# An RWKV time-mix stage in a whole-network kernel: one batch's recurrence levels issued between the last rounds of the stage before, the other's between outputs

## The chip, the cores and the metric

The kernel runs on one core of one Trainium2 chip. It computes a whole small network in one launch. The metric is the device time of that launch in microseconds (us), as the median of several runs. The core has TensorE (PE in the profile; PEld is its weight load), VectorE (DVE), ScalarE (ACT), GpSimd (POOL) and SyncE (SP, which here only issues DMAs). Each engine takes its own instructions strictly in the order in which they were built; engines wait for one another by semaphores.

## The reference, cut to what matters

The network is four residual blocks. The change lies in the first: an adapter with layer norm, then the RWKV time mix for 2 batches of 1024 tokens, 256 channels, 4 heads of 64. Everything is float32.

```
xx = shift(x) - x
m  = tanh((x + xx*maa_x) @ w1)                     # 4 x 32 wide
xw, xk, xv, xr = x + xx*(maa_f + m[f] @ w2[f])     # f in w, k, v, r
r, k, v = xr @ W_r, xk @ W_k, xv @ W_v
w = exp(-exp(decay + tanh(xw @ dw1) @ dw2))
# per head, over the tokens:
y_t = r_t @ (S + u * k_t v_t^T)
S   = diag(w_t) S + k_t v_t^T
out = groupnorm(y) @ W_o
x   = x + out
```

After it come a conditioned feed-forward layer ("cond2"), a mixture of experts, and two further blocks; they are not touched.

## The kernel before

**The front** is `tmix_in` (L261 to L375). The 2048 tokens are four chunks of 512 (`NCK` = 4, `CK` = 512); chunks 0 and 1 are batch 0, chunks 2 and 3 batch 1. Three generators work on a chunk: `adapt` (adapter and layer norm), `mix` (the four mixed inputs) and `project` (r, k, v and the decay w). Round i runs `adapt` on chunk i, `mix` on chunk i-1 and `project` on chunk i-2, and `together` (L253) takes their steps in the order of a string written out by hand:

```
together("apmpapmppaamppp", **steps)
```

So round 4 has only the mix of chunk 3 and the projection of chunk 2, and round 5 only the projection of chunk 3. r, k and v of batch 0 are complete after round 3. In `mix`, DVE multiplies each mixed input (L310) and POOL adds to it (L311), 4 of each for either half of the channels. In `project` the matmuls stand at L320 (decay), L328 (k and r), L336 (decay, second) and L346 (v); the front's PSUM is the pool "adp" (two banks "ad", one "nv", one "pa") and "mxp" (four banks f0 to f3).

**The recurrence** is `wkv` (L378 to L586). Each batch is cut into 8 pieces of 128 tokens. Within a piece the decayed products of r and k are built as a tree: a diagonal (L406; matmuls L414, times a mask by DVE at L422; its r is scaled by u on ACT at L560), then six levels with blocks of 1 to 32 tokens (L424). A level is 64 matmul instructions on 64x64 quarters of the array with 32 columns (L434, two records each in the profile). Its result is copied into A by DVE with a mask for levels 0 to 3 (L447, two copies of 512 columns per level), by ACT for levels 4 and 5 (L454). After each level comes a decay step (L456): POOL multiplies half of k (L462), DVE multiplies half of r (L463) and the running products `tot` (L465). The next level of the same batch needs the multiplied k and r. After the six levels `last` (L468) does the step between the two halves of a piece (matmuls L474, copies L482), with a decay as well. The two batches take turns at every level:

```
for l in range(6):
    for b in range(B):
        level(pp, b, l)
        decay(sp, b, l)
```

The levels use four PSUM banks named "sc".

**States and outputs.** `states` transposes k (L492, copied by ACT at L495), makes the state products (L509, copied at L516), and scans over the 8 pieces on DVE (L519). `output` (L522) makes y for two pieces at a time from A and v (L531) and from r and the states (L542); ACT copies one half out (L553), DVE adds the other (L554). `tmix_out` (L589) works on a chunk: square (L597), its sums (L602), the inverse root spread out (L607, L613), the normalized tile yn (L620, L621), and the output projection W_o (L626) added to x (L627). Its steps are taken in turn with the outputs, two steps after each. States of both batches come first, then the outputs of batch 0, then those of batch 1.

**After it** comes `cond2_0` (L635); its first matmul is at L654. Its weights, and those of the experts and their biases (L932), are loaded by DMAs that SP issues in the order of the program, each as soon as the memory that it writes is free.

Of the kernel before, what the change touches and what calls it, by code (L numbers as in the profile page):

```python
# [9 lines left out]
F32 = mybir.dt.float32  # L10
# [79 lines left out]
def setup(k, ctx):  # L90
    nc, tc, ins = k.nc, k.tc, k.ins
    cp = ctx.enter_context(tiles(tc, name="const", bufs=1))
    k.vecs = cp.tile([P, NVEC], F32, name="vecs")
    nc.sync.dma_start(out=k.vecs, in_=ins["vecs"])
    k.ident = cp.tile([P, P], F32, name="ident")
    make_identity(nc, k.ident)
    k.avg = cp.tile([P, P], F32, name="avg")
    nc.vector.memset(k.avg, 1.0 / C)

    k.sel64 = cp.tile([P, 2], F32, name="sel64")  # L100
    nc.vector.memset(k.sel64, 0.0)
    for h in range(2):
        nc.vector.memset(k.sel64[64 * h : 64 * h + 64, h : h + 1], 1.0 / 64)
    k.ones = cp.tile([P, P], F32, name="ones")
    nc.vector.memset(k.ones, 1.0)
    k.eps = {}
    for n, e in (("ln", 1e-5), ("gn", 0.00064)):
        k.eps[n] = cp.tile([P, 1], F32, name=f"eps_{n}")
        nc.vector.memset(k.eps[n], e)
# [134 lines left out]
def adapted(k, sp, pp, x, it, tables, names, hid):  # L244

    q = it["q"] = sp.tile([P, 2, CK + 1], F32, name="q", bufs=2)
    if it["ch"] % 2:
        k.nc.vector.tensor_copy(q[:, :, 0:1], it["prev"]["q"][:, :, CK : CK + 1])
    else:
        k.nc.vector.memset(q[:, :, 0:1], 0.0)  # L250
    yield from adapter_steps(k, sp, pp, x, it["ch"], q[:, :, 1:], tables, names, hid)
# [9 lines left out]
def tmix_in(k, x, r, kk, w, v):  # L261
# [10 lines left out]
    with (  # L272
# [4 lines left out]

        centre_weights(k, sp, ap, k.d0, D0, "wu", "bu")
# [4 lines left out]
        def adapt(it):  # L283
            return adapted(k, sp, ap, x, it, (k.d0, D0), ("wd", "wu", "bd", "bu"), P)
# [82 lines left out]
        for i in range(NCK + 2):  # L367
# [7 lines left out]
            together("apmpapmppaamppp", **steps)  # L375


def wkv(k, r, kk, w, v, y, x):  # L378
# [7 lines left out]
    NC = S // P  # L386
    M = NC - 1
    H = P // 2
    halves = [slice(i * H, i * H + H) for i in range(2)]
    with (  # L390
        tiles(tc, name="wka", bufs=1) as ap,
        tiles(tc, name="wkq", bufs=1, space=PSUM) as qp,
    ):
        eye = ap.tile([P, H], F32, name="eye")
        nc.vector.tensor_add(eye, k.ident[:, 0:H], k.ident[:, H:P])


        A = [ap.tile([P, 2, 2, NC, P], F32, name=f"A{b}") for b in range(B)]
        tot = [w[b].rearrange("p c t -> p (c t)") for b in range(B)]
        for b in range(B):  # L400
            nc.gpsimd.memset(A[b][halves[1], :, :, :, H:P].rearrange("p a c n t -> p (a c n) t"), 0.0)

        def bank(pp, shape):
            return pp.tile(shape, F32, name="sc", bufs=4)

        def diagonal(pp, b, ru):  # L406

            for c in range(2):
                ps = [bank(pp, [P, NC, H]) for par in range(2)]
                for ck in range(NC):  # L410
                    for half in range(2):
                        ts = slice(ck * P + half * H, ck * P + (half + 1) * H)
                        for par in range(2):
                            nc.tensor.matmul(  # L414
                                ps[par][halves[half], ck, :],
                                lhsT=kk[b][halves[par], c, ts],
                                rhs=ru[halves[par], c, ts],
                                start=True,
                                stop=True,
                            )  # L420
                for par in range(2):
                    nc.vector.tensor_mul(A[b][:, par, c, :, 0:H], ps[par], eye.unsqueeze(1).to_broadcast([P, NC, H]))  # L422

        def level(pp, b, l):  # L424

            h = 1 << l
            ps = [bank(pp, [P, 2, NC, H // 2]) for par in range(2)]
            for c in range(2):
                for ck in range(NC):
                    for half in range(2):  # L430
                        ts = slice(ck * P + half * H, ck * P + (half + 1) * H)
                        for par in range(2):
                            rv = r[b][halves[par], c, ts].rearrange("p (n two h) -> p n two h", two=2, h=h)
                            nc.tensor.matmul(  # L434
                                ps[par][halves[half], c, ck, :],
                                lhsT=kk[b][halves[par], c, ts],
                                rhs=rv[:, :, 1, :],
                                start=True,
                                stop=True,
                            )  # L440
            for par in range(2):
                dv = A[b][:, par, :, :, 0:H].rearrange("p c n t -> p (c n) t")
                dv = dv.rearrange("p g (n two h) -> p g n two h", two=2, h=h)[:, :, :, 1, :]
                pv = ps[par].rearrange("p c n t -> p (c n) t").rearrange("p g (n h) -> p g n h", h=h)
                if h < 16:
                    m = k.lvl[:, l].rearrange("p g (n h) -> p g n h", h=h)
                    nc.vector.copy_predicated(dv, m, pv)  # L447
                    continue

                for s0 in range(0, P, 32):  # L450
                    n = (s0 % H) // (2 * h)
                    if s0 % (2 * h) < h:
                        ss = slice(s0, s0 + min(h, 32))
                        nc.scalar.copy(dv[ss, :, n, :], pv[ss, :, n, :])  # L454

        def decay(sp, b, l):  # L456
            h = 1 << l
            n = 2 * S // (2 * h)
            t2 = tot[b].rearrange("p (n two) -> p n two", two=2)
            kv = kk[b].rearrange("p c (n two h) -> p (c n) two h", two=2, h=h)  # L460
            rv = r[b].rearrange("p c (n two h) -> p (c n) two h", two=2, h=h)
            nc.gpsimd.tensor_mul(kv[:, :, 0, :], kv[:, :, 0, :], t2[:, :, 1].unsqueeze(2).to_broadcast([P, n, h]))  # L462
            nc.vector.tensor_mul(rv[:, :, 1, :], rv[:, :, 1, :], t2[:, :, 0].unsqueeze(2).to_broadcast([P, n, h]))  # L463
            nt = sp.tile([P, n], F32, name=f"tot{l}", bufs=2)
            nc.vector.tensor_mul(nt, t2[:, :, 0], t2[:, :, 1])  # L465
            tot[b] = nt

        def last(pp, b):  # L468

            for c in range(2):  # L470
                ps = [bank(pp, [P, NC, H]) for par in range(2)]
# [11 lines left out]
            decay(ap, b, 6)  # L483

        def states(sp, b):
            kt = sp.tile([P, NC, C], F32, name="kt", bufs=1)
# [16 lines left out]
            pd = sp.tile([P, 2, H, M], F32, name="pd", bufs=1)  # L503
            for c in range(2):
                pu = qp.tile([P, NC, H], F32, name="pu")
# [16 lines left out]
        def output(sp, b, st, n):  # L522
# [28 lines left out]
            for a in range(2):  # L551
                t = sp.tile([P, 2, 2, H], F32, name="half")
# [3 lines left out]
        with tiles(tc, name="wks", bufs=2) as sp, tiles(tc, name="wkp", bufs=1, space=PSUM) as pp:  # L556
            for b in range(B):
                ru = sp.tile([P, 2, S], F32, name="ru")
                for c in range(2):
                    nc.scalar.activation(ru[:, c, :], r[b][:, c, :], AF.Copy, scale=k.vec("u", c))  # L560
                diagonal(pp, b, ru)
            for l in range(6):
                for b in range(B):
                    level(pp, b, l)
                    decay(sp, b, l)
            for b in range(B):
                last(pp, b)
        with (
            tiles(tc, name="wkt", bufs=2) as sp,
# [4 lines left out]
            before = [states(sp, b) for b in range(B)]  # L574
            left = []
            for b in range(B):
                for n in range(0, NC, 2):
                    output(sp, b, before[b], n)
                    for _ in range(2):
                        if left and next(left[0], 1):  # L580
                            left.pop(0)
                    if n % 4 == 2:
                        left.append(outs[(b * S + n * P) // CK])
            for steps in left:
                for _ in steps:
                    pass  # L586


def tmix_out(k, sp, pp, y, x, ch):  # L589
# [33 lines left out]
    for c in range(2):  # L623
        po = pp.tile([P, CK], F32, name="pw", bufs=2)
# [1164 lines left out]
def program(ctx: ExitStack, tc: tile.TileContext, ins, out):  # L1789
# [16 lines left out]
    with tiles(tc, name="w0", bufs=1) as wp:  # L1806
        load_adapter0(k, wp)
        with tiles(tc, name="rkwv", bufs=1) as ap:
            r, kk, w = ([ap.tile([P, 2, S], F32, name=f"{n}{b}") for b in range(B)] for n in "rkw")
            v = ap.tile([P, NBLK, C], F32, name="v")  # L1810
            with tiles(tc, name="zero", bufs=1) as zp:
# [11 lines left out]
                tmix_in(k, x, r, kk, w, v)  # L1823
            with tiles(tc, name="y0", bufs=1) as yp:
                y = yp.tile([P, 2, T], F32, name="y")
                wkv(k, r, kk, w, v, y, x)
# [138 lines left out]
```

## Time and profile before

| | |
|---|---|
| median of 3 runs | 1532.18 us (1529.52 to 1533.71) |
| the profiled execution | 1528.16 us |
| its span, first instruction to last | 1526.4 us |
| mean granted clock of PE | 0.959 |
| PE busy | 1426.0 us (93%) |
| DVE busy | 873.0 us (57%) |
| ACT busy | 680.4 us (45%) |
| POOL busy | 180.0 us (12%) |

A row of the profile's table of groups gives line, engine, operation, output and inputs by name, shape and count; then busy time and mean ns of one; then the idle time of the engine ahead of the group and what ended most of it. A line of the timeline gives start, duration, and the same; in brackets the idle time just before. "issue" is time for which no wait is seen. The granted clock is the share of full speed that PE was allowed. PE was at 1.00 from 50.7 us to 149.69, at 0.50 to 197.48, and at 1.00 to 224.79.

### The profile page before, as it was taken

Reading aid. Unit: us, or ns where it says so; the run is one execution under the profiler, and the core shown is the slowest. Engines: PE = TensorE matmul, PEld = TensorE weight load, DVE = VectorE, ACT = ScalarE, POOL = GpSimd, SP = SyncE. Lnnn points to the kernel's source line nnn. Section 1 sums busy time; section 2 is a strip of 40 time slices with the busy share of each in tenths; the row PEclk is TensorE's granted clock in tenths of the full one; section 3 lists DMA queues with packets and bytes.
Section 4 is the critical chain, followed back from the end, with each engine's and each line's share of the span. In section 5 each row is a group of like instructions: output and inputs, shape, how many; then the busy total and the mean of one; then the engine's idle time right before and its main releaser. Section 6 shows DMA issues by size and latency. Waiting matters only on the chain. (4 is left out here: it accounts for less than half of the span.)

```text
span 1526.4 us, 27470 instructions
## 1 busy us (share of the span) xinstructions
PE 1426.0 (93%) x10842; PEld 977.2 (64%) x10842; DVE 873.0 (57%) x2774; ACT 680.4 (45%) x1681; POOL 180.0 (12%) x167
## 2 busy tenths in 40 slices
PE   5998989999699999959999989999999999999998
PEld 2445977445456766736666545788887557878866
DVE  3545743121489921167888612788784237878764
ACT  2433242222122122127888621666574337656733
POOL 1533620022311111100000010000000000000011
PEclk9999589999799999979999999999999999999999
DMA  9500005200343342030000020000000000000001
GB/s 300 191 1 2 5 2 166 111 29 30 102 161 119 121 139 69 21 117 1 2 2 2 2 84 0 1 2 2 2 2 1 0 1 2 2 2 2 2 15 42
DMA packets 42759, 70.79 MB, mean 46 GB/s; under 512 B 7168, under 2 KB 35840, under 8 KB 39552
## 3 DMA queue, kind: packets, MB, share of 16 engines
q1 hardware_dynamic: 35776, 55.55, 10.9%
q0 software_dynamic: 3072, 8.65, 1.6%
q10 hardware_dynamic: 3776, 4.75, 1.0%
q8 instruction: 88, 1.44, 0.4%
q14 instruction: 47, 0.39, 0.1%
HBM read 45.09 MB, written 23.86 MB: 45 GB/s over the span
## 5 line engine op out<-in xcount | busy, mean ns | idle before, releaser
L1624 ACT ACTIVATE pe<-pe,nm 128x320 f32<-128x320 f32 x256 | 141.8, 555 | 131.2 <-DVE nm L1614 131.0
L1614 DVE CUSTOM_DVE_ANT_0 pe<-ps,wbs 128x320 f32<-128x320 f32 x256 | 118.6, 487 | 6.1 <-PE ps L1608 1.8
L1236 ACT ACTIVATE pe<-pe,nm 128x256 f32<-128x256 f32 x256 | 110.4, 498 | 20.4 <-DVE nm L1226 20.4
L971 PE MATMUL ph<-xt,w 128*128 128x512 f32 x256 | 113.8, 602 | 2.7 <-ACT xt L966 2.7
L1604 PE MATMUL ps<-kT,qT 64*128 64x384 f32 (+1 forms) x512 | 110.2, 498 | 3.4 <-DVE qT L1578 2.9
L979 PE MATMUL po<-w,h 128*128 128x256 f32 x512 | 111.8, 379 | 0.0
L979 PEld LDWEIGHTS po<-w,h 128*128 128x128 f32 x512 | 97.3, 190 | 16.6 <-issue 3.1
L1226 DVE CUSTOM_DVE_ANT_0 pe<-ps,lc 128x256 f32<-128x256 f32 x256 | 94.2, 417 | 20.9 <-PE ps L1210 19.3
L1673 PE MATMUL py<-ptt,v 128*64 128x128 f32 x1408 | 103.6, 277 | 0.1
L901 DVE SCALAR_TENSOR_TENSOR lc<-iok,idx,lc 128x256 f32<-128x256 f32 x248 | 102.3, 478 | 0.3
L971 PEld LDWEIGHTS ph<-xt,w 128*128 128x128 f32 x256 | 48.5, 193 | 62.7 <-issue 55.8
L1673 PEld LDWEIGHTS py<-ptt,v 128*64 128x64 f32 x1408 | 78.7, 137 | 11.1 <-issue 8.3
L1646 PE MATMUL pt<-ident,pe 128*128 128x128 f32 x512 | 79.8, 281 | 1.9 <-DVE pe L1632 0.9
L1245 PE MATMUL ptp<-ident,pe 128*128 128x128 f32 x512 | 73.7, 283 | 5.7 <-ACT pe L1236 3.1
L1245 PEld LDWEIGHTS ptp<-ident,pe 128*128 128x128 f32 x512 | 55.8, 142 | 33.1 <-ACT pe L1236 16.8
L974 ACT ACTIVATE h<-ph,vecs 128x512 f32<-128x512 f32 x64 | 44.0, 687 | 72.0 <-PE ph L971 71.0
L1633 ACT ACTIVATE pe<-pe,rd 128x320 f32<-128x320 f32 x128 | 70.7, 558 | 9.0 <-DVE rd L1631 8.9
L1608 PEld LDWEIGHTS ps<-sk,qT 64*128 64x128 f32 x512 | 50.9, 187 | 26.1 <-issue 0.3
L1505 PE MATMUL pq<-c,w1ak 128*128 128x512 f32 x128 | 61.7, 625 | 5.3 <-ACTq L1850 5.3
L1653 DVE TENSOR_TENSOR ptt<-pt,tri 128x512 f32<-128x512 f32 x96 | 64.9, 676 | 0.0
L1646 PEld LDWEIGHTS pt<-ident,pe 128*128 128x128 f32 x512 | 56.2, 141 | 10.9 <-issue 2.0
L982 DVE TENSOR_TENSOR ye<-po,b 128x256 f32<-128x256 f32 x32 | 13.4, 420 | 81.7 <-PE po L979 81.7
(355 smaller groups left out, 2764.7 us busy)
## 6 DMA issues: line engine op xcount, KB each, us to landing
w<-in_mw SPq DMA_DIRECT2D x16, 1024.0 KB, 5.1
xs<-z SPq DMA_DIRECT2D x8, 1088.0 KB, 11.8
ys<-z SPq DMA_DIRECT2D x4, 1024.0 KB, 11.6
xe<-xs SPq DMA_DIRECT2D x7, 544.0 KB, 6.2
more<-xs SPq DMA_DIRECT2D x7, 544.0 KB, 5.5
x<-in_xT ACTq DMA_DIRECT2D x4, 512.0 KB, 6.3
g<-ys ACTq DMA_DIRECT2D x4, 512.0 KB, 6.3
out_x<-o SPq DMA_DIRECT2D x8, 256.0 KB, 2.1
```

Of the source, the lines that this page charges most:

```text
L901: nc.vector.scalar_tensor_tensor(n, key, k.idx[:, qb, j : j + 1], n, ALU.is_equal, ALU.add)
L971: nc.tensor.matmul(ph, lhsT=w1[:, c, m * P : (m + 1) * P], rhs=xt[:, c, :], start=c == 0, stop=c == 1)
L979: nc.tensor.matmul(po, lhsT=h[:, m, j * P : (j + 1) * P], rhs=w2[:, m, :], start=m == 0, stop=m == 7)
L1226: nc.vector.tensor_tensor_reduce(out=pe[:, j, :], in0=it["ps"][i][:, j, :], in1=k.lc[:, q0 + j, :], scale=-1.0, scalar=3.0e38, op0=ALU.add ...
L1236: nc.scalar.activation(pe[:, j, :], pe[:, j, :], AF.Exp, bias=nm, scale=-1.0)
L1245: nc.tensor.transpose(ptp[:, kb, j, :], it["pe"][i][:, j, kb * P : (kb + 1) * P], k.ident)
L1604: nc.tensor.matmul(ps[:, i, keys[i]], lhsT=qs[i], rhs=kT[hp, m + pair, k0 : k0 + nk], start=True, stop=True)
L1614: nc.vector.tensor_tensor_reduce(out=pe[:, i], in0=ps[:, i, used[i]], in1=wbs[:, 0 if n == 0 else 3 if n == NB - 1 else 1 + i, (1 - i) * G ...
L1624: nc.scalar.activation(pe[:, i], pe[:, i], AF.Exp, bias=nm[:, i : i + 1], scale=-1.0, accum_out=den[:, i : i + 1])
L1633: nc.scalar.activation(pe[:, 1], pe[:, 1], AF.Copy, scale=rd[:, 1:2])
L1646: nc.tensor.transpose(pt[1 - j if i and inner(n) else j][:, 2 * pair + i, :], pe[:, at : at + P], k.ident)
L1673: nc.tensor.matmul(py[64 * i : 64 * i + 64, (m + pair) % 4, :], lhsT=keys[:, hs], rhs=it["pts"][:, pair, :] if j == 3 else it["pt"][:, j, ...
```

## The change

- The front takes steps of batch 0's recurrence as a fourth generator, `w`, in rounds 4 and 5, with an order of its own for each. Eight steps in all: two halves of the diagonal, six levels. They use the adapter's two "ad" banks, and the adapter's scratch memory is given up for the generator's `ru` and `tot` at round 4.
- In `wkv` only batch 1's levels are left. The first three steps (diagonal, diagonal, level 0) come first, then `last` of batch 0, level 1, `states` of batch 0, and then levels 2 to 5, each followed by one output of batch 0. Then come `last`, `states` and the outputs of batch 1.
- "sc" has two banks where it had four; the state products share the bank "pk" with the transposes; the output projection's "pw" has one bank where it had two. The scratch of states has one buffer where it had two, and batch 1's `ru` lies in the second half of y.
- The products `tot` alternate between w's memory and one more buffer, and stand right behind each level's decay.
- The small matrix `eye` is made at the start; A of batch 0 is allocated and cleared ahead of the front.

```diff
-def tmix_in(k, x, r, kk, w, v):
+def tmix_in(k, x, r, kk, w, v, A):
...
-        centre_weights(k, sp, ap, k.d0, D0, "wu", "bu")
+        beside = ExitStack()
+        dp = beside.enter_context(tiles(tc, name="ads", bufs=1))
+        centre_weights(k, dp, ap, k.d0, D0, "wu", "bu")
...
-            together("apmpapmppaamppp", **steps)
+            if i < NCK:
+                together("apmpapmppaamppp", **steps)
+                continue
+            if i == NCK:
+                beside.close()
+                dp = beside.enter_context(tiles(tc, name="wk0", bufs=1))
+                ru, tot = dp.tile([P, 2, S], F32, name="ru"), dp.tile([P, S], F32, name="tot")
+                levels = wkv_levels(k, r[0], kk[0], w[0], A, ru, tot, lambda shape: ap.tile(shape, F32, name="ad", bufs=2))
+            together("pwmpwmpwmpwppwpp" if i == NCK else "pwpwpwppppp", w=levels, **steps)
+        beside.close()
+def wkv_decay(k, r, kk, bufs, l):
+    nc = k.nc
+    h = 1 << l
+    n = 2 * S // (2 * h)
+    t2 = bufs[l % 2][:, 0 : 2 * n].rearrange("p (n two) -> p n two", two=2)
...
+    nc.gpsimd.tensor_mul(kv[:, :, 0, :], kv[:, :, 0, :], t2[:, :, 1].unsqueeze(2).to_broadcast([P, n, h]))
+    nc.vector.tensor_mul(rv[:, :, 1, :], rv[:, :, 1, :], t2[:, :, 0].unsqueeze(2).to_broadcast([P, n, h]))
+    nc.vector.tensor_mul(bufs[(l + 1) % 2][:, 0:n], t2[:, :, 0], t2[:, :, 1])
+def wkv_levels(k, r, kk, w, A, ru, tot, bank):
...
+    for c in range(2):
+        nc.scalar.activation(ru[:, c, :], r[:, c, :], AF.Copy, scale=k.vec("u", c))
+    for c in range(2):
...
+        yield
+    for l in range(6):
...
+        wkv_decay(k, r, kk, (w.rearrange("p c t -> p (c t)"), tot), l)
+        yield
...
+        def bank(shape):
+            return lp.tile(shape, F32, name="sc")
...
-                pu = qp.tile([P, NC, H], F32, name="pu")
+                pu = qp.tile([P, NC, H], F32, name="pk")
...
-        with tiles(tc, name="wks", bufs=2) as sp, tiles(tc, name="wkp", bufs=1, space=PSUM) as pp:
-            for b in range(B):
-                ru = sp.tile([P, 2, S], F32, name="ru")
-                for c in range(2):
-                    nc.scalar.activation(ru[:, c, :], r[b][:, c, :], AF.Copy, scale=k.vec("u", c))
-                diagonal(pp, b, ru)
-            for l in range(6):
-                for b in range(B):
-                    level(pp, b, l)
-                    decay(sp, b, l)
-            for b in range(B):
-                last(pp, b)
...
-            before = [states(sp, b) for b in range(B)]
...
+            ru = y[:, :, S : 2 * S]
+            levels = wkv_levels(k, r[1], kk[1], w[1], A[1], ru, ap.tile([P, S], F32, name="tot"), bank)
             for b in range(B):
+                for _ in range(3):
+                    next(levels, 1)
+                last(b)
+                next(levels, 1)
+                st = states(sp, b)
                 for n in range(0, NC, 2):
-                    output(sp, b, before[b], n)
-                    for _ in range(2):
-                        if left and next(left[0], 1):
-                            left.pop(0)
+                    next(levels, 1)
+                    output(sp, b, st, n)
+                    rest(2)
                     if n % 4 == 2:
                         left.append(outs[(b * S + n * P) // CK])
...
-        po = pp.tile([P, CK], F32, name="pw", bufs=2)
+        po = pp.tile([P, CK], F32, name="pw")
```

The bodies of the diagonal and of a level in `wkv_levels` are those of `diagonal` and `level` before.

## The prediction
> **What bounds the kernel now.** I read the page first, for where TensorE (PE) is not busy or not at full clock. The rows are tenths in 40 slices of 38.2 us:
>
> ```profile
> PE   5998989999699999959999989999999999999998
> PEclk9999589999799999979999999999999999999999
> ```
>
> PE is the bound nearly everywhere. The lowest clock of the whole span is in the fifth slice (152.6 to 190.8 us), which is the recurrence. Second, the table of 20 us windows round it (columns: us, busy us and instructions of PE, PEld, DVE, ACT, POOL, then granted clock, DMA share, GB/s):
>
> ```profile
> 100.00:120.00 20.00, 19.91 (x62) 9.23 (x61) 9.57 (x13) 7.81 (x15) 7.37 (x7) 1.00 0.00 0
> 140.00:160.00 20.00, 15.34 (x672) 14.29 (x664) 17.00 (x25) 1.32 (x2) 8.08 (x3) 0.74 0.02 4
> 160.00:180.00 20.00, 18.89 (x658) 18.16 (x659) 16.86 (x16) 0.15 (x1) 10.65 (x5) 0.50 0.02 4
> 180.00:200.00 20.00, 18.42 (x518) 17.62 (x517) 9.56 (x10) 12.64 (x29) 16.08 (x6) 0.56 0.02 5
> 200.00:220.00 20.00, 16.84 (x291) 13.48 (x285) 7.39 (x9) 8.57 (x17) 3.56 (x3) 1.00 0.01 2
> ```
>
> The front (first row) keeps PE full at clock 1.00 and leaves DVE and POOL half idle. The levels hold PE over 90% busy and the clock at 0.50, so "PE busy" is half empty there. Third, the timeline of the levels (start, us, what; idle before):
>
> ```profile
> 147.28 2.07 PE L434 MATMUL sc<-r,k 64*64 64x32 f32 x128 [1.03 <-issue]
> ...
> 151.63 2.51 DVE L447 COPY_PREDICATED A<-lvls,sc 128x512 f32<-128x512 uint8 x2
> 151.64 2.85 POOL L462 TENSOR_TENSOR k<-k,w 128x1024 f32<-128x1024 f32 x1 [1.02 <-PE sc L434]
> ...
> 153.92 1.65 DVE L463 TENSOR_TENSOR r<-r,w 128x1024 f32<-128x1024 f32 x1
> 155.82 3.63 PE L434 MATMUL sc<-r,k 64*64 64x32 f32 x128 [0.49 <-issue]
> ...
> 171.15 3.64 PE L434 MATMUL sc<-r,k 64*64 64x32 f32 x128 [0.19 <-issue]
> ```
>
> A level is 128 records: 2.07 us at full clock, 3.64 at half. Behind it lie 2.5 us of masked copy and 1.65 of the r product in turn on DVE (4.2 us), and beside them 2.85 on POOL: one batch's next level can start about 4.2 us after this one's end. Two batches in turn hide that now (level of one, 3.6, behind the other's vector work), which is why little idle is charged:
>
> ```profile
> L434 PE MATMUL sc<-r,k 64*64 64x32 f32 x1536 | 41.9, 280 | 5.5 <-issue 4.8 <-DVE r L463 0.4 <-DVE A L422 0.3
> L462 POOL TENSOR_TENSOR k<-k,tot 128x1024 f32<-128x1024 f32 x12 | 31.1, 2596 | 16.4 <-PE sc L434 14.9 <-PE sc L474 1.4
> ```
>
> **The stage in numbers.** Round 4 of the front starts on PE at 102.25, the front ends at 136.4, the recurrence to 199.2, and the first matmul of the next stage (L654) is at 274.5: 34.15 + 62.8 + 75.3 = 172.25 us. All that the change moves is in this stretch. The changed kernel has the same matmuls; its order on each engine does show levels between front matmuls and between outputs, so "it does not do what it says" is excluded.
>
> **Part 1, batch 0's levels in rounds 4 and 5.** PE work: front 34.15; two diagonal halves at 1.04 and six levels at 1.9 (the 2.07 less its last drain), 13.5. Waits: PE takes its instructions in order, so a front matmul behind a level waits for its own operands too. Where the second half of k waits for the mixed value xv, its DVE step (L310, 0.74) stands before the level: 1.5. Behind level 0 stand the masked copies and r product (4.2) on DVE, and behind them the L310 step of xw; the matmuls that need it wait about 3.1. Levels 1 and 2 wait for the r product: 0.9 + 0.55. Level 5 waits for POOL's k product (2.95, L462) and ACT's copies (3.0, L454): 1.5. Sum 7.5. In round 4 POOL also adds the mixed values (8 x 1.09, L311), and the k product queues with them; the wait for it is in these sums. Front end: 102.25 + 34.15 + 13.5 + 7.5 = 157.4. Below this bound: no wait at all, 149.9. Above: each half-clock window of 3.4 us adds up to 1.7; I take 1.1, so 158.5.
>
> **Part 2, batch 1's levels with batch 0's outputs.** PE work at full clock: diagonals 2.1, levels 11.4, last of batch 0 (64 records) 1.9, transposes and state matmuls 4.9, four output blocks at 2.9 = 11.6, chunk 0's norm (1.95 + 2.1) and projection 3.7: 39.6. Waits: the scaled copy ru on ACT 1.55; two PSUM banks where there were four, so each diagonal half waits for the copies out (L422, 0.65 each), about 2; level 0 to last to level 1 stand behind the same 4.2 us DVE chain with only last's 1.9 between, about 4.2; the state scan, shown below, 2.1; level 3 behind level 2's masked copy and r product, which queue after the scan on DVE, 1.5. Sum 11.4, stage 51.
>
> ```profile
> 206.83 2.02 DVE L519 TENSOR_TENSOR_SCAN st<-td,pd 128x896 f32<-128x896 f32 x1 [2.40 <-ACT pd L516]
> ```
>
> **The clock in Part 2 decides most.** At half clock its PE work grows: levels 6 x 1.7 = 10.4, diagonals and last 4, outputs 4 x 1.7 = 6.8 (estimated at 1.6 times), transposes and norms about 4; some 25, of which waits absorb 3: 22. The trace gives both ends: the levels alone ran at half clock for 47.8 of their 62.8 us (149.69 to 197.48); outputs and states held 1.00 from 197.48 to 224.79 although PE waited there. The woven stream lies between. By array use (a 64-column stream of the last step brought the clock back at 197.48, the 32-column levels never did) I am nearer the outputs' row: an output or norm block stands in nearly every 3.4 us window behind the scan, the levels before it have none. I take 6 of the 22.
>
> The Trainium skill bears on this twice. TensorE: Matmul & The Clock Gate, "Why this matters for your kernels", asks for over 4 us of busy PE for full clock and no idle gap over about 3 us. By that rule the old levels, 94% busy, would be at 1.9 us each; the row shows 3.64 at clock 0.50, so busy time is not what is counted here, and a level is priced by the row. The other speaks against the change: the section on psum-queue depth-cycling says that short waits on banks taken in turn make the clock swing; by it the halved banks would give nearly all of the 22, and the sum would end at +9. The row against it is 200 to 220: 16.84 of 20 busy, many short waits, clock 1.00. I weigh the row more.
>
> **Part 3, the rest to L654.** Last of batch 1 1.9, POOL's k product 3.2 (L462; nothing covers it now that the other batch is through), states 9.7 (199.18 to 208.9), four outputs 11.6, chunks 1 and 2 2 x 7.7 = 15.5, chunk 3's norm 2 and the tail to L654 10.8 as now, less 2 because chunk 2's projection falls into the norm wait: 52.5.
>
> **Small parts.** The eye (0.21, L395), the memsets of A (1.8 each on POOL) move to idle engines: 0, cover is the start and the front; 2 at most if not. The tot products stay on DVE, now right behind each level's r product (1.2 falling to 0.1): hidden, up to 1 in Part 1. The single bank of the projection ("pw") makes its second half wait for a 0.7 us add: between 0 and 3 over four chunks; 0.5. SP's queue: the next stage's weights wait on the last transposes, and the bias load of L932 and those behind it now wait for the last normalized tile, some 4.5 us before L654. Main weights land about 10 us before their use; the small ones may hold ACT by 0 to 3; PE has three banks to go on; I take 0.5.
>
> **Sum.** 158.5 + 51 + 6 + 52.5 + 1 = 269 against 274.5; bounded by 245 (no waits in Part 1, three quarters of those in Part 2 gone, full clock) and 290 (all half clock in Part 2, all small parts at their upper ends). Gain 5.5, and with Part 1's waits likelier too high than low (DVE was charged a whole chain each time) I take 7. Against the profiled execution's own 1528.16 (span 1526.4 and 1.8 round it) that is 1521; it lies 4 below the median of the runs, so on the median 1525.
>
> **Rivals.**
> *Full clock kept, waits as summed or smaller.* 157.4 + 51 + 52.5 = 261, gain 13.5; up to 20 with half of Part 1's waits: 1512 to 1519. For it: the outputs' row at 1.00. Against: PE is in order and DVE near its limit in 140 to 180 (17 of 20).
> *Slower: half clock over the whole of batch 1's levels.* 158.5 + 51 + 22 + 52.5 + 1 = 285, 10.5 late: 1542. Its place is from the first diagonal to the last output of batch 0. It turns slower when more than 11.5 of the 22 come, that is over about half of that stretch. For it: waits of 11.4 in 51 us lower the array use, and levels never brought the clock back. Against: the outputs' row.
> *Nothing net.* What is hidden in the front returns as waits of PE behind DVE and POOL, one batch alone having no partner: Part 1's waits 7.5 become 14: 1532.
>
> **Numbers.** The likeliest case 0.35 (1520 to 1530), full clock 0.22, slower 0.30, nothing net 0.13. A measurement of this kernel tells about 0.3% (4.6 us) from no change. Faster: 0.22 + 0.28 of the likeliest = 0.50. Same: 0.07 + 0.10 = 0.17. Slower: 0.30 + 0.03 = 0.33. The range reaches from the middle of the full-clock case to the slower one's price: 1511 to 1542.
>
> **What would show it.** L654 at about 268. Front end at 158, with PE idle charged to DVE xw L310 near level 0. Between there and batch 0's last output, clock about 0.85; near 0.55 the slower case holds, at 1.00 the full one. PE idle charged to the r product and to the scan, together about 11. If L654 comes as said but the total differs, the loads behind SP's queue are late: the first FFN stage would then wait for its weights. Most wrong I would be if level matmuls between wide ones cost more than 1.9 at full clock: two pauses charged to "issue" (1.03 and 1.66 us, at 147.28 and 151.01) are not explained by any wait in the trace, and one per level would cost 12.

## The result, and the profile after

| | before | changed |
|---|---|---|
| median | 1533.71 us (1527.22 to 1539.74, 11 runs) | 1545.01 us (1539.38 to 1552.25, 11 runs) |
| profiled execution, its span | 1528.16, 1526.4 | 1548.84, 1547.1 |
| mean granted clock | 0.959 | 0.952 |

The ratio is 1.0082, with a 95% interval of 1.0063 to 1.0102: about 12.6 us slower, where 7 faster was forecast. The time is past the rival called slower (1542), and outside the range.

The page of the changed kernel, 40 slices of 38.7 us:

```profile
PE   5998888999969999969999989999999999999998
PEclk8789768999979999979999999999999999999999
```

The single slice at 5 is gone, but the loss is spread: 7, 6 and 8 in slices five to seven, and lower digits in the first three as well. So I divided the trace where the prediction did. Round 4 now starts on PE at 113.02, the front ends at 173.15, batch 0's last output at 237.17, and the first matmul of the next stage (L676 now) is at 298.0. Columns as before; the first row is the recurrence in the kernel before, the others are the three parts of the changed kernel:

```profile
136.40:199.20 62.80, 53.73 (x1922) 51.16 (x1921) 44.55 (x54) 17.47 (x33) 34.01 (x14) 0.62 0.02 4
...
113.02:173.15 60.13, 53.04 (x997) 31.20 (x995) 32.53 (x40) 19.44 (x35) 25.46 (x15) 0.94 0.01 2
173.15:237.17 64.02, 53.90 (x1304) 49.59 (x1303) 30.94 (x40) 18.36 (x35) 21.85 (x9) 0.68 0.01 3
237.17:298.00 60.83, 52.90 (x503) 37.78 (x503) 21.88 (x38) 15.51 (x30) 6.85 (x13) 0.86 0.24 75
```

From the start of round 4 to L676 (called the stretch from here on) it is 185.0 us, where it was 172.25 in the trace of before. Part 1 took 60.1 (56.25 said), Part 2 64.0 at clock 0.68 (57 said), Part 3 60.8 (52.5 said). Besides, everything starts 10.8 us later (113.02 against 102.25), in rounds where no matmul was moved. From L676 to the end the changed kernel is 2.8 us shorter (1249.1 against 1251.9).

"Half clock" below is time at granted clock 0.50, added up from the trace's record of the clock: 6.8 us in Part 1, 41.0 in Part 2 and 17.1 in Part 3. What PE waited for in Part 2 (engine, line, waited for: us in total, times, longest):

```profile
PE py L566 <- DVE st L543: 1.9, 1, 1.9
PE sc L497 <- DVE A L457: 1.5, 1, 1.5
PE pk L516 <- ACT kt L519: 1.4, 2, 0.7
PE sc L444 <- issue: 1.2, 1, 1.2
PE sc L424 <- ACT y L416: 1.1, 1, 1.1
```

With those left out they come to 10.0 us, against 11.4 in my sum. In sum the waits were forecast well, though not one by one: level 3's wait for the r product (1.5) isn't there, the chain from level 0 over `last` to level 1 gave 2.0 where 4.2 was said, and the transposes' 1.4 was not in the sum. PE's own work was not forecast well. Its groups in Part 2:

```profile
L444 PE MATMUL sc<-r,k 64*64 64x32 f32 x768 | 21.0, 264 | 2.1 <-issue 1.2 <-DVE A L432 0.8
...
L497 PE MATMUL sc<-r,k 64*64 64x64 f32 x64 | 5.9, 316 | 2.0 <-DVE A L457 1.5 <-ACT A L505 0.5
```

Six levels (L444) took 21.0 us, 3.5 each, where I had put 1.9. In the front the same six took 14.1. The timeline of the front shows both the price of a woven level and the waits:

```profile
124.09 1.98 PE L332 MATMUL f<-xk,wa 128*128 128x512 f32 x4 [1.66 <-DVE xv L314]
...
132.74 3.62 PE L332 MATMUL f<-xr,wa 128*128 128x512 f32 x4 [3.73 <-DVE xw L314]
...
150.57 2.07 PE L444 MATMUL ad<-r,k 64*64 64x32 f32 x128
...
161.46 2.95 PE L444 MATMUL ad<-r,k 64*64 64x32 f32 x128 [1.28 <-POOL k L404]
```

A level between wide matmuls runs in 2.07 us and pays no pause to "issue"; front matmuls wait 1.7 and 3.7 us for DVE, as forecast (1.5 and 3.1); the 3.62 lies in a half-clock window (132.94 to 136.36), and the 2.95 reaches into one (163.66 to 167.08).

### The profile page after: what moved, and what is told of

Read it like the earlier page. It is cut to its first block, busy times and chain, and to the rows that moved or that the text cites. A ratio compares the mean times of both kernels' runs of the same rounds, so it can differ in the third digit from the quotient of the medians.

```text
span 1547.1 us, 27450 instructions
## 1 busy us (share of the span) xinstructions
PE 1438.0 (93%) x10842; PEld 977.8 (63%) x10842; DVE 875.9 (57%) x2774; ACT 681.3 (44%) x1681; POOL 183.0 (12%) x167
## 3 DMA queue, kind: packets, MB, share of 16 engines
q1 hardware_dynamic: 35776, 55.55, 10.7%
## 6 DMA issues: line engine op xcount, KB each, us to landing
ys<-z SPq DMA_DIRECT2D x4, 1024.0 KB, 10.8
```

## The experiments

Theories: **clock** (the loss is half clock where levels are mixed with other work, the forecast's rival), **lost partner** (a batch alone has nothing to put behind its own copies and products), **banks** (two PSUM banks where there were four), and for the late start of round 4 a **draw of the clock** (it differs from one execution to the next) against a **cost of the change**. A run's ratio to the kernel before is uncertain by about 0.2%, so a difference of two ratios by some 4 us; where that hides the effect, the stretch in the trace is given beside it (185.0 in the changed kernel). Traces repeat better where nothing was touched: Part 2 took 64.0, 64.1 and 63.8 us in the changed kernel and in the runs "the mix ahead" and "Tile A cleared late" below, Part 3 took 60.8, 60.9 and 59.8.

**Batch 1's levels alone.** In `wkv`:

```diff
+            for _ in range(8):
+                next(levels, 1)
             for b in range(B):
-                for _ in range(3):
-                    next(levels, 1)
                 last(b)
-                next(levels, 1)
+            for b in range(B):
                 st = states(sp, b)
                 for n in range(0, NC, 2):
-                    next(levels, 1)
                     output(sp, b, st, n)
```

> The changed kernel, but batch 1's levels stand alone again: diagonal and all six levels one after another, then last of both batches, then states and outputs batch by batch. Only the weave with the front is left of the change. Theory 'clock' (the loss is that PE runs at half clock in the stretch of batch 1's levels): the stretch stays at half clock, so about the time of the changed kernel, 1545 to 1550. Theory 'lost partner' (a batch alone has no work to put behind its own copy, r product and k product, about 4.2 us a level): each level alone costs 6.5 to 8 us where a pair cost 7.5 for two, the front's gain stays, and the sum is 1550 to 1560, with PE idle before every level charged to the r product. Both say slower than the changed kernel; the size and the idle time tell them apart.

1566.96, ratio 1.0224 (1.0204 to 1.0244), stretch 204.5. That is past what either theory said; lost partner (1550 to 1560) is the nearer one, and PE waits 15.0 us for the r product in four waits, as it said.

**Batch 0's levels alone.** The orders become "pmppmppmppp" and "ppppppppwwwwwwww".

> The changed kernel, but batch 0's diagonal and levels stand alone behind the front, none within rounds 4 and 5. Only the weave with the outputs is left. 'Lost partner': batch 0's levels cost about 7 us each, 45 us behind a front of 34, so 20 us over the changed kernel, near 1565. 'Clock': levels at 3.64 and little more, 25 to 30 us behind the front, against the 26 that they cost in it: about 1545 to 1550.

1568.22, ratio 1.0244 (1.0225 to 1.0264), stretch 208.2. Its waits behind the front:

```profile
PE ad L444 <- DVE r L405: 14.9, 4, 4.2
PE ad L444 <- POOL k L404: 3.2, 1, 3.2
```

Levels of the lone batch started at 157.87, 165.33, 172.48 and 179.53, so 7.1 to 7.5 us apart, of which 3.4 to 4.2 was waiting for the r product. A pair cost about that much for both batches. Lost partner gave these numbers (7 us a level, 1565), clock did not. The whole lone batch runs at half clock (148.49 to 240.65), which is where its 3.64 us of PE a level come from; the waits come on top. By the ratios, issuing batch 1's levels between outputs is worth some 22 us against leaving them alone, and issuing batch 0's between front matmuls some 25; what the change has to beat is the pair.

**Banks given back.** For the diagonal, level 0 and `last` of batch 0 the pairs of banks alternate with the outputs' two; the norm's sum moves into the bank "nb" and "pw" has two:

```diff
-            return lp.tile(shape, F32, name="sc")
+            i = taken[0] % 4
+            taken[0] += 1
+            if i < 2 or taken[0] > 10:
+                return lp.tile(shape, F32, name="sc")
+            return qp.tile(shape, F32, name=f"py{i - 2}")
...
-    pv = pp.tile([P, nb * 4], F32, name="nv")
+    pv = pp.tile([P, CK], F32, name="nb")[:, 0 : nb * 4]
...
-        po = pp.tile([P, CK], F32, name="pw")
+        po = pp.tile([P, CK], F32, name="pw", bufs=2)
```

> The changed kernel with PSUM banks given back: batch 1's diagonal, level 0, last of batch 0 and level 1 take turns over four banks (the outputs' two banks are free then), and the projection has two banks again, the norm's small sum sharing one with the normalizing product. Theory 'banks' (two banks instead of four make PE wait): 4 to 6 us faster than the changed kernel, 1540. 'Clock' and 'lost partner': within 2 us of it, 1543 to 1546.

1537.48, ratio 1.0043 (1.0021 to 1.0065), stretch 175.3. Part 1 stayed at 60.1; Part 2 fell from 64.0 to 57.7, and Part 3 from 60.8 to 57.5:

```profile
167.50:225.23 57.73, 48.76 (x1303) 43.93 (x1303) 30.67 (x40) 18.34 (x35) 22.69 (x9) 0.73 0.01 3
225.23:282.70 57.47, 50.08 (x504) 37.99 (x504) 21.79 (x38) 15.50 (x30) 6.85 (x13) 0.88 0.33 108
```

All banks together were worth 9.7 us in the trace, 6 by the ratios. The four banks act in Part 2 and gave 6.3 there; I had put them at 2. PE's idle time in Part 2 fell only from 10.1 to 9.0 us; its busy time fell by 5.1, with half clock down from 41.0 to 30.7 us. How much of this is the clock and how much the denser order, this run doesn't part; nor does it part, in Part 3, the projection's second bank from a half clock of 13.7 us where there had been 17.1.

**Added matmuls to hold the clock.**

```diff
+            def heat(n):
+                po = gp.tile([P, CK], F32, name="pw")
+                for _ in range(n):
+                    nc.tensor.matmul(po, lhsT=k.ident, rhs=v[:, 0:2, :].rearrange("p a c -> p (a c)"), start=True, stop=True)
...
                     next(levels, 1)
+                    if b == 0:
+                        heat(2)
                 last(b)
+                if b == 0:
+                    heat(2)
```

and two more behind level 1 and behind the states, one before each output.

> The changed kernel with 16 added matmuls of 128x128 by 512 columns (0.86 us each at full clock, 13.7 us in all, results unused) between the steps of batch 1's levels and of batch 0's last and states, to keep the array in use. 'Clock': full clock from the front's end to batch 0's outputs; 41 us of half clock are worth 13 us, some 9 of the 13.7 lie in waits, so 5 to 9 us faster than the changed kernel, 1536 to 1540. 'Lost partner': the clock is at full too, but the chain of copy and products sets the pace, so the added matmuls give nothing or cost 3 to 8 us, 1545 to 1553.

1540.81, ratio 1.0060 (1.0042 to 1.0078); the changed kernel's interval overlaps, so by time alone a gain of 3 is likely, not shown. Part 2 in the trace:

```profile
170.28:230.36 60.08, 57.28 (x1336) 42.71 (x1334) 31.62 (x40) 18.17 (x35) 21.78 (x9) 0.91 0.01 3
```

and the levels' group there:

```profile
L444 PE MATMUL sc<-r,k 64*64 64x32 f32 x768 | 15.8, 233 | 1.5 <-DVE r L405 1.5
```

With 13.7 us of useless work (16 times 0.86 us, an estimate) Part 2 became 3.9 shorter, and half clock in it fell from 41.0 to 10.2 us. PE's busy time less the added work is 43.6 where it was 53.9, so the lower clock cost some 10.3 us there, against 6 in the forecast. It may be more: the trace has the added matmuls busy for 18.8 us, part of it beside other work. The levels fell from 21.0 to 15.8.

**The kernel before, with one added matmul behind each level.**

> The kernel before, with one added matmul of 128x128 by 512 columns (0.86 us at full clock, result unused) behind each of the 12 levels, 10.3 us in all. 'Clock': the levels' 47.8 us at half clock go to full, each level from 3.64 to 2.0 and the added 0.86: up to 9 us faster, 1524. 'Something else paces a dense level stream' (at full clock levels started 3.6 to 3.7 us apart in before, at 143.7, 147.28 and 151.0, with pauses charged to issue): no gain, 1532 to 1543, although the granted clock is at 1.00.

1535.19, ratio 1.0018 (0.9997 to 1.0039): no difference to be told, though the stretch in its trace is 177.2 (the first levels still ran at half clock, where an added matmul shows 2.07 us, not 1.12). This is the timeline at granted clock 1.00 (L558 is the added matmul):

```profile
174.08 1.81 PE L434 MATMUL sc<-r,k 64*64 64x32 f32 x107
177.14 0.54 PE L434 MATMUL sc<-r,k 64*64 64x32 f32 x21 [1.25 <-issue]
177.61 1.13 PE L558 MATMUL py<-v,ident 128*128 128x512 f32 x2
178.67 1.76 PE L434 MATMUL sc<-r,k 64*64 64x32 f32 x105
180.97 0.55 PE L434 MATMUL sc<-r,k 64*64 64x32 f32 x23 [0.54 <-issue]
181.45 1.12 PE L558 MATMUL py<-v,ident 128*128 128x512 f32 x2
```

With added matmul and all, a level starts 3.8 us after the last one (178.67 to 182.50; 3.6 to 3.9 in those that follow, 3.1 and 4.6 in the two ahead), where it was mostly 3.7 to 4.1 at half clock without it. PE pauses inside each level for no wait that the trace names. So a dense level stream is not paced by the clock alone: the "clock" theory falls for the old levels, and "PE busy is half empty there" was wrong as a promise.

The record of DMA packets shows what these pauses go with. The instruction queue q8 brings one packet of 16 KB for each level. Here its packets landed at 175.72, 179.52, 183.43, 186.89, 190.49 and 194.04, and the pauses ended at 177.14, 180.97, 184.79, 188.34, 191.89 and 195.47, each 1.4 us later. It is so for all 33 pauses charged to "issue" between 100 and 285 us in the traces of both kernels and of every run here: each ended 1.2 to 1.6 us after such a packet had landed. In the front of the changed kernel the packets come 5 to 10 us apart, and there is no such pause. So what paces the dense levels is in all likelihood the fetching of their instructions, about 3.7 us a level, and that would be why full clock bought them nothing in this run. No run varied the fetching, and none has dense levels at full clock throughout without added work; the few at the start of the old kernel's levels start 3.1 to 4.0 us apart in three traces, where DVE's copy and r product take over 4 us a level as well.

**The kernel before once more,** unchanged.

> The kernel before once more, unchanged, for a second look at its first 110 us. In the trace of before, round 4 of the front starts at 102.25 us, in those of the changed kernel and its variants between 107 and 113, though none of them changes an instruction order of PE in rounds 0 to 3. 'Draw of the clock' (these microseconds are set by which 3.4 us windows fall to half clock early on, and come and go with any kernel): round 4 starts anywhere from 102 to 113 here, and the stretch from there to the first matmul of the next stage is 172 again to within 2 us. 'Cost of the change' (the cleared A and the eye at the start delay the front): 102 again.

Round 4 started at 110.53 and the stretch was 168.8, in an execution of 1532.88. Half clock before round 4 was 30.7 us, where the first trace of before has 13.7 and that of the changed kernel 37.5. In the run with one added matmul behind each level, whose front is that of before, round 4 started at 106.18 with 23.9 us of half clock. So most of the 10.8 us is a draw; it comes with the kernel before too, and may be much of why either kernel's runs spread over some 13 us. The stretch of before is 169 to 172.

**The late step of batch 1 early:** `last(1)` directly behind the last output of batch 0.

> The changed kernel, but batch 1's last step stands right behind batch 0's last output, ahead of the norm and projection of chunk 0, not behind them. In the changed kernel POOL's k product of that step starts 8 us after that output and the transposes wait 2.7 us for it. 'The late last step costs': the states of batch 1 begin some 5 us earlier, the norms fill the wait, 2 to 4 us faster than the changed kernel, 1541 to 1543. Rival, 'PE is full there anyway' (what is moved forward only pushes the rest back): within 1.5 us of 1545.

1542.99, ratio 1.0051 (1.0027 to 1.0076), stretch 178.5. The interval overlaps that of the changed kernel. In the trace Part 3 fell from 60.8 to 55.4, with half clock down from 17.1 to 6.8 us:

```profile
230.18:285.58 55.40, 48.65 (x494) 34.58 (x490) 20.21 (x38) 15.43 (x30) 6.30 (x13) 0.94 0.26 83
```

The wait that the edit was made for hardly moved. Here it is in the changed kernel, then in this run:

```profile
PE pk L516 <- POOL k L404: 2.7, 1, 2.7
...
PE pk L516 <- POOL k L404: 2.3, 1, 2.3
```

PE's busy time fell by 4.2 us and its idle time by 1.2, so the gain is mostly the clock. Over the eight traces that leave both batches' levels where the change put them, Part 3 follows half clock: 55.4 and 55.6 us where it held 6.8, 57.5 where it held 13.7, and 58.5 to 60.9 where it held 17.1. One of the latter has the early step too (the first of the two sums below), so why half clock was shorter here stays open.

**The mix ahead of the levels:** round 4's order becomes "pmwpmwpmwpwppwpp".

> The changed kernel with one string changed: in round 4 each step of the mix stands ahead of the level step, not behind it, so that DVE empties the front's banks before it takes the level's copy and r product. In the changed kernel PE waits 1.7 and 3.7 us there for DVE. If these waits are lost time: 4 to 5.4 us faster than the changed kernel, 1540. If the wait only moves to the level that follows (for the r product or k product, now behind the mix on DVE and POOL): 0 to 2 us.

1542.08, ratio 1.0064 (1.0046 to 1.0083), not told apart by time. Part 1 fell from 60.1 to 58.3: the waits of 3.7 and 1.7 are down to 0.4, and waits for POOL's k product rose from 1.3 to 3.9. Half of the wait only moved, as the second half of the expectation had it.

**Tile A cleared late:** the clearing of A0 takes its zeros from r, which is there only after round 2.

```diff
+            if i == 3:
+                for par in range(2):
+                    for c in range(2):
+                        zero = A[HALVES[1], par, c, :, 64:P]
+                        old = r[0][HALVES[1], c, 0:512].rearrange("p (n t) -> p n t", n=WC)
+                        nc.gpsimd.tensor_scalar_mul(zero, old, 0.0)
...
-            nc.gpsimd.memset(A[HALVES[1], :, :, :, 64:P].rearrange("p a c n t -> p (a c n) t"), 0.0)
```

> The changed kernel, but A of batch 0 is cleared after round 2 of the front (as r times zero, which is there only then), not on POOL in the first 3 us. In the changed kernel the order on DVE in the first rounds is another than before: the centring of W_v (reduce, a small product that takes 2.30 us there where it took 0.17, and a subtraction) stands ahead of the adapter's first subtraction, which starts at 19.67 us where it started at 17.32. 'The early clear costs': with the old order back, the first round's PE work is about 2.2 us earlier and the whole is 2 us faster than the changed kernel, 1543. Rival 'draw of the clock': no difference beyond 1 us, since the front's spread of 10 us comes from the clock.

1540.43, ratio 1.0058 (1.0035 to 1.0081), by time alone not told apart from the changed kernel either; stretch 185.35: what it gives lies ahead of round 4. The adapter's first norm on PE starts at 23.75, where it was 26.35 in the changed kernel and 23.81 and 24.18 in the two traces of before. Over all traces here it starts at 25.0 to 26.65 with the early clear (eight) and at 23.46 to 24.67 without it (five), so the early clear costs 1 to 3 us. The cause is on DVE and POOL in the changed kernel:

```profile
16.26 2.74 POOL L131 COPY lvls<-lvl 128x3072 uint8<-128x3072 uint8 x1 [9.53 <-DMA lvl<-in_lvl]
...
16.73 2.30 DVE L367 TENSOR_SCALAR wvm<-wvm 128x8 f32<-128x8 f32 x1
...
19.67 1.28 DVE L214 TENSOR_TENSOR y<-x,ad 128x512 f32<-128x512 f32 x2
```

and in the kernel before:

```profile
17.32 1.28 DVE L212 TENSOR_TENSOR y<-x,ad 128x512 f32<-128x512 f32 x2 [2.62 <-PE ad L209]
...
19.24 0.17 DVE L363 TENSOR_SCALAR wvm<-wvm 128x8 f32<-128x8 f32 x1
```

With POOL's clear in the first 3 us the order built for DVE has the centring of W_v ahead of the adapter's subtraction. An 8-column product then takes 2.30 us, not 0.17, and ends at 19.03, just as POOL's copy ends (19.00). In the run with an added matmul behind each level the same product started later under POOL's copy, at 18.47: it took 0.60 us and ended at 19.07, where the copy ended at 19.04. The Trainium skill (SBUF — State Buffer, "SBUF: two separate sides") says that POOL and some DVE instructions, a tensor_scalar like this one possibly among them, take a shared pair of ports as an exclusive lock, and that the one that comes second stands still until the first is through; these rows agree.

**Together.** The four banks, the early last step, the mix ahead and the late clear; the norm's and the projection's banks as in the changed kernel. First the first three alone, with the norm's bank shared and the projection's second bank:

> Three edits together on the changed kernel: the four banks and the projection's second bank (7 us faster alone), the last step of batch 1 early, the mix ahead of the levels. If the three are independent and as large as hoped: 7 + 3 + 4.5, 1530, some 2 to 3 us faster than the kernel before. If only the banks count: 1537. Loss of the partner as a limit would show as a stretch (from round 4 to the next stage) that stays above the 172 us of before.

1533.65, ratio 1.0001 (0.9982 to 1.0020), stretch 175.2. Its third part was 58.5 us, and PE waited 2.6 us there for the spread root (DVE nl). Without the sharing and the second bank, and with the late clear (the 61.9 and 54.4 in the next lines divide the trace some 3 us ahead of batch 0's last output; divided at it, these parts are 58.5 and 57.7):

> On the changed kernel: four banks in turn for the first steps of batch 1, last step of batch 1 early, mix ahead of the levels, A of batch 0 cleared late; the norm's sum and the projection's banks as in the changed kernel (in the run with them shared, the third part was 61.9 us where the early last step alone gave 55.4). If the parts add: 56.9 in rounds 4 and 5, 54.4 to 56.4 to batch 0's last output, 55.4 to the next stage, together 168 where the kernel before has 169 to 172, and 2 us each from the early front and from what follows: 1526 to 1529, 4 to 6 faster than before. If sharing was not the cause of the 61.9: 1532.

1528.32, ratio 0.9971 (0.9957 to 0.9984): 4.4 us faster than the kernel before.

```profile
107.08:163.91 56.83, 52.52 (x997) 31.18 (x995) 32.27 (x40) 19.19 (x35) 26.44 (x15) 0.94 0.01 2
163.91:221.09 57.18, 46.84 (x1318) 42.59 (x1319) 31.78 (x40) 18.34 (x35) 20.33 (x9) 0.76 0.01 3
221.09:276.70 55.61, 48.77 (x495) 34.53 (x490) 20.21 (x38) 15.43 (x30) 6.29 (x13) 0.94 0.26 81
```

All three parts are below those of the changed kernel; the stretch is 169.6. The third part is 55.6, the 55.4 that was hoped for. By the ratios the edits alone give 6.0, 4.8, 2.8 and 3.7 us, each uncertain by some 4, in sum 17.3; together 17, which is clear. The stretch alone is no shorter than the shorter one of before (168.8); what follows it is 4.1 us shorter than in the traces of before (1247.8 against 1251.9), about as much as the whole gain.

## Why the prediction was wrong

**The stage and its three parts** held, and so, roughly, did the reading that nothing outside moves much (1 to 3 us by the change ahead of it, 2.8 behind it). That the changed order is really there was right too.

**Part 1** came out 3.9 us over. The waits were right, 6.9 against 7.5, and so was their place. Half-clock windows came to 6.8 us where 2.2 were assumed, and the levels' PE time was 14.1 where 11.4 stood in the sum.

**Part 2** failed, in the term "levels 11.4" and in "I take 6 of the 22". Chunk 0's projection (3.7) fell into Part 3, so on its own ground Part 2 was 64.0 against 53.3, 10.7 over. Waits were 1.4 less than said. By the run with added matmuls the clock cost about 10.3 in place of 6, and PE's work with the clock nearly full was 43.6 where 35.9 was said, on the estimate of 0.86 us for each added matmul; the six levels alone took 21.0, and 15.8 with the clock at 0.91. The pause per level that I named as the place where I might be most wrong was not it: Part 2 has one, of 1.2 us. The wrong choice was to weigh the outputs' row (clock 1.00) more than the levels': the run of outputs begins 38 us into Part 2 (211.40), and until then it is mostly levels, `last` and transposes one after another, as before. The trace had that order to be read. The other ground was that the 64-column last step brings the clock back; here the last step of batch 0 (186.72 to 193) ran at half clock throughout. Half clock held 41.0 of the 64 us, past the half at which my slower rival decided, so that rival had the place right. That its 1542 is near the 1545 is in part luck: it took all 22 us for the clock in Part 2, which makes 69.3 without the projection where 64.0 came, and Parts 1 and 3 made up for it with 3.9 and 4.6 more than said.

**The price of the halved banks** was put at 2 us of waits; giving them back took 6.3 off Part 2 in the trace, more than half of the 10.7. The Trainium skill's section on psum-queue depth-cycling (TensorE: Matmul & The Clock Gate), which I set aside for one row of the outputs, named this side: half clock in Part 2 fell by 10.3 us with the four banks. By the ratios all banks together are 6 us of the time, and how much of that is by the clock is not parted.

**Part 3** was 4.6 over without that projection. It had no term for the clock, and half clock lasted 17.1 us. The wait for the k product, which I had put at 3.2, was 2.7. In the run with the early last step Part 3 was 5.4 shorter, with that wait still 2.3 and half clock at 6.8.

**Small parts:** the clear of A was put at 0, "2 at most if not". It cost 1 to 3, not by its own 1.8 us, but by the order that it changed on DVE.

**What is behind the sign.** In before, the diagonals and levels of both batches take 54.3 us (136.4 to 190.7), 27.2 for each, and `last` of both takes 8.5. In the front, batch 0's diagonal and levels cost 60.1 less 34.1, or 26.0: 1.2 gained. What is left costs 124.8 (Parts 2 and 3) less the 75.3 of states, outputs and tail, or 49.5, where batch 1's levels and `last` of both took 35.6: 13.9 lost. That is the 12.7 by which the stretch grew. The early clear added 1 to 3, and what follows L676 gave back 2.8. It is 1 to 4 us shorter in every trace of the changed kernel and its variants (1247.7 to 1250.8, where before has 1251.8 to 1251.9), which I did not trace to a cause. The sum is near the 12.6 of the ratio. In the last version the same sums are 4.5 gained and 1.9 lost; against the second trace of before (168.8) the stretch gains nothing, and the 4.4 us by the ratio would lie behind L676.

## What to carry to other kernels

A stretch at half clock isn't a reserve until something shows that its stream would run faster at full; the spacing of starts where the clock happened to be full (3.6 and 3.7 us at 143.71 to 151.01 in before) hinted at it here. When two independent chains hide each other's latency, moving one of them elsewhere must be priced for the one left behind, which here lost 13.9 us where the moved one gained 1.2. Buffers given up to make room, and a small clear put early, change orders and waits far from where they stand, so each is worth a run of its own.

## What the hardware showed that I had not expected

- A dense stream of small matmuls (128 records and as many weight loads a level) mostly starts a level every 3.7 to 4.1 us at clock 0.50, and at 1.00 it takes an added matmul a level at a spacing of mostly 3.6 to 3.9. Between wide matmuls a level takes 2.07. The pauses that the trace calls "issue" end 1.2 to 1.6 us after a 16 KB instruction packet has landed, one packet a level; that the fetching sets the pace is likely and was not tested.
- An 8-column DVE product took 2.30 us while POOL copied, 0.17 otherwise; begun later under the same copy, 0.60. It ended with the copy each time.
- The first 110 us of the same kernel differ by 8 us between executions (102.25 and 110.53) with half-clock windows of 13.7 and 30.7 us.
